# Two-layer graph attention: score rows spread by GpSimd's broadcast in place of transfers from HBM, and the deviation by log, exp and a Newton step

## The chip, the cores and the metric

The kernel runs on one core of one Trainium2 chip. The metric is the device time in microseconds. A profile is one further execution, recorded by the hardware profiler; its span is a little longer than the timed median.

## The reference

A batch of 32 graphs with 512 nodes and 512 features each. The input is normalized by rows, passed through a relu and then through two layers of graph attention, and the result is added to the input. Cut to what matters:

```python
def gat_layer(x, mask, W, a_src, a_dst, bias, concat):
    xl = (x @ W).reshape(B, N, H, F)
    asrc = jnp.einsum('bnhf,hf->bnh', xl, a_src)
    adst = jnp.einsum('bnhf,hf->bnh', xl, a_dst)
    e = jax.nn.leaky_relu(asrc[:, :, None, :] + adst[:, None, :, :], 0.2)
    e = jnp.where(mask[..., None], e, -1e9)
    attn = jax.nn.softmax(e, axis=1)                    # over the sources
    out = jnp.einsum('bsdh,bshf->bdhf', attn, xl)
    return (out, heads joined or averaged) + bias

h = relu((x - mean(x)) / sqrt(var(x) + 1e-5))           # by rows
h = elu(gat_layer(h, mask, W1, ...))                    # 4 heads of 256
return x + gat_layer(h, mask, W2, ...)                  # 1 head of 512
```

The mask is `adj > 0` with the diagonal added. All is float32.

## The kernel before, in words

All 32 graphs are worked one after the other, with up to three in flight at once. For each graph the kernel does this:

- `load` (L548) and `norm` (L586) bring in x and compute mean and deviation by rows: bn_stats and bn_aggr on VectorE, then the power -0.5 of variance plus epsilon on GpSimd (L597), which takes a constant tile `half`. `norm_turn` (L606) applies it with a relu on ScalarE and turns the tile, from the third graph on through a transposing transfer (`x<-adj`, L637) with a copy on ScalarE before and after it.
- `masks` (L555) makes a mask of 0 and a large negative number in `m`, writes it to HBM (`dm`) and turns it (`mt`).
- `project1` and `project2` (L962, L1158) are the products with the weights, and `gather1` and `gather2` (L1079, L1251) the products with the attention. They work by a scheme of seven half-size products in place of eight, so that VectorE forms sums and differences of blocks (`hs`, `t`, `p`, `xl`, `h`), and PSUM (`mm`) is emptied by ScalarE and VectorE. Matmuls are recorded under L439.
- The scores of a layer are in `Soft` (L657). For each destination `first` (L710) adds the source scores to a destination's score, with the leaky relu (ScalarE, `l<-as,z`), applies the turned mask and takes the largest (VectorE, `l<-l,mt`), and sums the exponentials (ScalarE, `l<-l,low`); from that come two rows per head. `second` (L763) then builds the attention with the sources on the partitions: VectorE takes the larger of two sums of these rows (`p<-rr,z`), GpSimd issues an accumulating transfer that adds the mask from HBM (`p<-dm`, L433, two per head), and ScalarE takes the exponential (`p<-p,z`).

**The spread.** In two places a vector that lies with 128 nodes down the partitions has to become one long row that every partition holds: the source scores (tile `as`, two heads at once, or one in layer 2) and the two rows of the softmax (tile `rr`, once per head). Both go through `Soft.spread` (L665). VectorE transposes the vector in blocks of 32 (`as<-z`, `rr<-low`), a small transfer writes it to HBM (`das<-as`, `drr<-rr`), and a second one reads it back to all 128 partitions (`as<-das`, `rr<-drr`). Per graph there are three spreads of scores and five of softmax rows, most of them 1024 elements long. There are two `as` tiles and two `rr` tiles. The readers are ScalarE (`l<-as,z`) and VectorE (`p<-rr,z`).

**What sets the order of the work.** Nothing is issued while the functions run: each operation is added to a `Program` (L87) with an engine, a price in us, what it reads and writes, and for transfers a size in us. `order` (L234) then plans all engines together and emits the instructions in the planned order. Every engine runs its own list strictly in that order. TensorE's list is the order of the calls; the others are chosen by rank. Waits between engines are priced by

```python
CROSS, SAME = 0.15, 0.07
PAIRS = {("PE", "ACT"): 0.21, ("PE", "DVE"): 0.21, ("DVE", "POOL"): 0.58, ("POOL", "DVE"): 0.4}
DMA_LEAD, DMA_TAIL, AHEAD = 0.8, 2.0, 3.5
```

and jobs of SyncE and GpSimd are held back while the planned transfers run more than `AHEAD` us behind (L220). The plan knows nothing of one engine holding up another at the memory. So a change of one price or of one operation moves instructions everywhere on ScalarE, VectorE, GpSimd and SyncE. Operations are recorded under the helpers' lines: ScalarE L422, VectorE L425, transfers of SyncE L428, accumulating transfers of GpSimd L433.

Of the kernel before, what the change touches and what calls it, by code (L numbers as in the profile page):

```python
# [10 lines left out]
F32 = mybir.dt.float32  # L11
# [3 lines left out]
AF = mybir.ActivationFunctionType  # L15
OP = mybir.AluOpType
# [3 lines left out]
P = 128  # L20
EPS = 1e-5
# [277 lines left out]
def tile_gat(  # L299
# [36 lines left out]
    nc = tc.nc  # L336
# [4 lines left out]
    NT = N // P  # L341
# [9 lines left out]
    sbuf = ctx.enter_context(tc.tile_pool(name="sbuf", bufs=1))  # L351
# [6 lines left out]
    def slots(name, n, shape, dtype=F32, pool=sbuf):  # L358
# [4 lines left out]
    make_identity(nc, identf)  # L363
    diag = sbuf.tile([P, P], BF16, name="diag")
    nc.vector.tensor_scalar(diag, identf, -1.0, BIG, op0=OP.add, op1=OP.mult)
    half = sbuf.tile([P, NT], F32, name="half")
    nc.vector.memset(half, -0.5)

# [19 lines left out]
    m = sbuf.tile([P, NT, N], BF16, name="m")  # L390
# [17 lines left out]
                tensor=w1_sb.tensor, offset=w1_sb.offset + NT * (DO + 2) + i * NT * N,  # L408
                ap=[w1_sb.ap[0], [N, NT], [1, N]],
# [9 lines left out]
    prog = Program()  # L419

    def act(cost, reads, writes, *a, **k):
        prog.add("ACT", cost, reads, writes, lambda: nc.scalar.activation(*a, **k))  # L422

    def dve(cost, reads, writes, f, *a, **k):
        prog.add("DVE", cost, reads, writes, lambda: f(*a, **k))  # L425

    def dma(size, reads, writes, to, at, cost=0.4):
        prog.add("SP", cost, reads, writes, lambda: nc.sync.dma_start(to, at), size)  # L428
# [15 lines left out]
    COPY, ADD, TINY = 0.28, 0.34, 0.1  # L444
# [141 lines left out]
    def norm(b):  # L586
        sk, st = stats.take()
        S, A = nc.vector.BN_STATS_DIM, nc.vector.BN_AGGR_DIM
        for t, (xk, xt) in enumerate(XT[b]):
            dve(0.61, [xk], [sk + (t,)], nc.vector.bn_stats, st[:, t, :S], xt)  # L590
            dve(TINY, [sk + (t,)], [sk + (t,)], nc.vector.bn_aggr, st[:, t, S : S + A], st[:, t, :S])
        every = [sk + (t,) for t in range(NT)]
        rstd = st[:, :, S + A]
        dve(TINY, every, every, nc.vector.tensor_scalar_add, rstd, st[:, :, S + 1], EPS)
        prog.add(
            "POOL", 1.0, every, every,
            lambda: nc.gpsimd.tensor_tensor(rstd, rstd, half, op=OP.pow),  # L597
        )
        shift = st[:, :, S]
        dve(  # L600
            TINY, every, every, nc.vector.scalar_tensor_tensor,
            shift, shift, -1.0, rstd, op0=OP.mult, op1=OP.mult,
        )
        ST[b] = sk, st
# [52 lines left out]
    class Soft:  # L657
# [7 lines left out]
        def spread(self, v, keys, rows, to, through, n=NT):  # L665

            k = rows * n
            ok, o = to.take()
            dk, dr = through.take()

            c = 32 // k
            sb = o[:, 0, :32]
            dve(
                0.12, keys, [ok], nc.vector.transpose,
                sb, bass.AP(tensor=v.tensor, offset=v.offset, ap=[v.ap[0], [1, k], [0, c]]),
            )
            dma(
                0.03, [ok], [dk], dr[:k].rearrange("k (b j) -> b k j", j=32),
                bass.AP(
                    tensor=sb.tensor, offset=sb.offset, ap=[[c * sb.ap[0][0], P // c], [1, 32]]  # L680
                ),
                0.55,
            )
            dma(
                0.18 * rows * n, [dk], [ok], o[:, :rows, : n * P],
                bass.AP(tensor=dr.tensor, offset=dr.offset, ap=[[0, P], [n * P, rows], [1, n * P]]),
            )
            through.give(dk)
            return ok, o

        def columns(self, i, given=None):

# [173 lines left out]
    def sevens(left, right, rkeys, put, kh, units, width, order, seeds={}):  # L866
# [3 lines left out]
        for us, n in order:  # L870
# [30 lines left out]
            if n in (2, 3, 4):  # L901
# [17 lines left out]
                tensor=hs.tensor, offset=hs.offset + KQ * M,  # L919
                ap=[hs.ap[0], [KH * M, 2], [M, 2], [1, M]],  # L920
# [398 lines left out]
    load(0)  # L1319
    weights1()  # L1320
    norm(0)
    for t in range(NT):
        norm_turn(0, t)
# [3 lines left out]
    run(project1_first(given))  # L1327
    load(1)
    norm(1)
    for t in range(NT):  # L1330
        norm_turn(1, t)
# [16 lines left out]
    for h in gather1_plain(S1[0], range(H)):  # L1348
# [8 lines left out]
        if h == 2:  # L1357
            s.second(1)
    load(2)
    norm(2)  # L1360
    s.first(2)
    s.first(3)
# [8 lines left out]
    for i in range(B - 1):  # L1371
# [17 lines left out]
        if front:  # L1389
# [5 lines left out]
            n = S1[i + 2] = Soft(i + 2, 1, scores_1)  # L1395
# [69 lines left out]
```

## Time and profile before

The time is 2844.79 us, the median of three runs from 2837.85 to 2845.18. The profiled execution has a span of 2856.3 us.

| from the page | value |
|---|---|
| packets of all transfers | 501.42 MB, mean 176 GB/s |
| queue q1 (SyncE's transfers) | 332.15 MB, 42.5% of 16 engines' span |
| queue q0 (GpSimd's transfers) | 166.74 MB, 25.6% |
| rr<-drr | 159 transfers of 512 KB and 2 of 256 KB |
| as<-das | 64 transfers of 512 KB and 32 of 256 KB |
| p<-dm | 314 transfers of 512 KB, median 5.6 us to landing |
| VectorE p<-rr,z, 128x512 | 740 ns mean, 636 times (some shorter) |
| VectorE l<-l,mt, 128x512 | 682 ns mean, 640 times |
| GpSimd stats<-stats,half | 1512 ns mean, 32 times |

How to read it: a busy share is busy time over the span. In a line of a group or a wait, `p<-rr,z` means that the instruction writes tile p and reads rr and z, and `engine line <- other` means that the engine stood idle before its instruction until the other was done. PE is TensorE, DVE VectorE, ACT ScalarE, POOL GpSimd and SP SyncE. The chain of waits is followed back from the last instruction, at each step to what released it. Since each engine's list is fixed, a late landing also delays everything that stands behind the instruction that waits for it.

### The profile page before, as it was taken

How to read it: one execution, taken by the hardware profiler on the slowest of the kernel's cores; microseconds unless marked ns; L12 is line 12 of the kernel's file. 1: busy time of each engine (PE TensorE's matmuls, PEld its weight loads, DVE VectorE, ACT ScalarE, POOL GpSimd, SP SyncE). 2: the span in 40 equal slices, each digit the busy share in tenths (PEclk: the TensorE clock that was granted, in tenths of full speed). 3: DMA queues.
4: the chain of work that ended last, by engine and by line, in shares of the span. 5: the costliest groups of instructions: out<-in, count | busy, mean ns of one | idle time of the engine just before them, and what ended most of it. 6: DMA issues, size and time to landing. Idle time of an engine off the chain costs nothing.

```text
span 2856.3 us, 39591 instructions
## 1 busy us (share of the span) xinstructions
PE 2770.0 (97%) x12520; PEld 2373.9 (83%) x12520; DVE 2432.2 (85%) x5494; ACT 2384.9 (83%) x4506; POOL 322.6 (11%) x356
## 2 busy tenths in 40 slices
PE   7999999999999999999999999999999999999988
PEld 6688888888888888888888888888878888888876
DVE  7888898888898878879889888888878988888885
ACT  5888898878898888878888888888878898888882
POOL 0111111101111101111011100111101111111110
PEclk9999999999999999999999999999999999999999
DMA  7666767666777667776687776777666767666652
GB/s 226 153 176 167 204 161 188 181 174 170 189 188 177 176 166 196 167 173 179 172 181 167 196 155 184 170 176 197 164 168 178 195 174 178 183 183 177 176 141 96
DMA packets 369077, 501.42 MB, mean 176 GB/s; under 512 B 220260, under 2 KB 225124, under 8 KB 368868
## 3 DMA queue, kind: packets, MB, share of 16 engines
q1 hardware_dynamic: 323076, 332.15, 42.5%
q0 software_dynamic: 45792, 166.74, 25.6%
q8 instruction: 100, 1.64, 0.2%
q14 instruction: 109, 0.89, 0.1%
HBM read 315.89 MB, written 51.31 MB: 129 GB/s over the span
## 4 chain that ended last, share of the span: by engine, by line
PE 79%; DMA 9%; ACT 5%; DVE 5%; issue 2%; SPq 0%; POOL 0%; ACTq 0%; POOLq 0%; DVEq 0%
PE mm L439 79%; DMA p<-dm 4%; DMA x<-adj 3%; DVE p L425 1%; ACT l L422 1%; ACT p L422 1%; DMA as<-das 1%; ACT adj L422 1%; ACT ht L422 1%; DVE l L425 1%; DVE t L425 1%; DVE hs L425 1%; DVE h L425 1%; ACT xl L422 0%; ACT xr L422 0%
## 5 line engine op out<-in xcount | busy, mean ns | idle before, releaser
L439 PE MATMUL mm<-w_sb,hs 128*128 128x257 f32 (+2 forms) x3032 | 685.3, 383 | 25.1 <-ACT h L422 16.1
L439 PEld LDWEIGHTS mm<-w_sb,hs 128*128 128x128 f32 x3032 | 576.1, 191 | 120.7 <-ACT h L422 20.1
L433 POOL DMA_DIRECT2D p<-dm x314 | 274.4, 878 | 2420.4 <-DVE p L425 1459.7
L422 ACT ACTIVATE l<-l,low 128x512 f32<-128x512 f32 x640 | 455.2, 713 | 40.0 <-DVE low L425 39.3
L439 PE MATMUL mm<-w_sb,ht 128*128 128x258 f32 x2112 | 482.6, 382 | 3.6 <-ACT ht L422 1.4
L425 DVE CUSTOM_DVE_ANT_1 l<-l,mt 128x512 f32<-128x512 f32 x640 | 425.2, 682 | 62.8 <-ACT l L422 62.2
L422 ACT ACTIVATE p<-p,z 128x512 f32<-128x512 f32 (+1 forms) x636 | 424.7, 709 | 62.3 <-DMA p<-dm 51.2
L439 PE MATMUL mm<-p,xl 128*128 128x256 f32 (+1 forms) x1984 | 470.6, 385 | 4.5 <-ACT h L422 3.0
L422 ACT ACTIVATE l<-as,z 128x512 f32<-128x512 f32 x640 | 436.9, 712 | 32.0 <-DMA as<-das 30.7
L439 PE MATMUL mm<-w_sb,h 128*128 128x257 f32 x2056 | 459.5, 380 | 3.3 <-DVE w_sb L425 3.3
L425 DVE SCALAR_TENSOR_TENSOR p<-rr,z 128x512 f32<-128x512 f32 (+1 forms) x636 | 448.1, 740 | 15.8 <-DMA rr<-drr 15.1
L439 PEld LDWEIGHTS mm<-w_sb,ht 128*128 128x128 f32 x2112 | 398.8, 190 | 67.6 <-ACT xl L422 3.3
L439 PEld LDWEIGHTS mm<-w_sb,h 128*128 128x128 f32 x2056 | 390.3, 190 | 62.3 <-DVE w_sb L425 3.7
L439 PEld LDWEIGHTS mm<-p,xl 128*128 128x128 f32 x1984 | 377.8, 191 | 68.0 <-issue 6.9
L422 ACT ACTIVATE xr<-h,b_sb 128x512 f32<-128x512 f32 x248 | 171.8, 714 | 120.9 <-DVE h L425 120.9
L422 ACT ACTIVATE xl<-mm 128x516 f32<-128x516 f32 (+2 forms) x376 | 218.4, 586 | 46.9 <-PE mm L439 45.6
L439 PE MATMUL mm<-t,hs 128*128 128x256 f32 x992 | 233.1, 386 | 25.0 <-ACT mm L422 22.0
L439 PEld LDWEIGHTS mm<-t,hs 128*128 128x128 f32 x992 | 189.7, 193 | 57.5 <-ACT mm L422 27.1
L425 DVE SCALAR_TENSOR_TENSOR h<-h,b_sb,xr 128x512 f32<-128x512 f32 x248 | 181.5, 744 | 46.5 <-ACT xr L422 46.4
L422 ACT ACTIVATE ht<-x 128x1024 uint16<-128x1024 uint16 x120 | 159.3, 1351 | 30.2 <-DMA x<-adj 30.2
L439 PE MATMUL mm<-xl,p 128*128 128x256 f32 (+1 forms) x752 | 180.2, 388 | 2.3 <-DVE t L425 1.6
L422 ACT ACTIVATE h<-mm 128x512 f32<-128x512 f32 (+1 forms) x256 | 146.3, 574 | 26.5 <-PE mm L439 24.4
(113 smaller groups left out, 3268.0 us busy)
## 6 DMA issues: line engine op xcount, KB each, us to landing
p<-dm POOLq DMA_DIRECT2D x314, 512.0 KB, 5.6
rr<-drr SPq DMA_DIRECT2D x159, 512.0 KB
x<-in_x_dram SPq DMA_DIRECT2D x128, 256.0 KB
adj<-in_adj_dram SPq DMA_DIRECT2D x128, 256.0 KB
as<-das SPq DMA_DIRECT2D x64, 512.0 KB
t<-in_x_dram SPq DMA_DIRECT2D x62, 512.0 KB
out_dram<-t SPq DMA_DIRECT2D x60, 512.0 KB
dm<-m SPq DMA_DIRECT2D x32, 512.0 KB
```

The source lines that it names most:

```text
L422: prog.add("ACT", cost, reads, writes, lambda: nc.scalar.activation(*a, **k))
L425: prog.add("DVE", cost, reads, writes, lambda: f(*a, **k))
L433: lambda: nc.gpsimd.dma_start(to, at, accum_op=OP.add), size,
L439: f(*a, **k)
```

## The change

In `spread` the row is read back from HBM into one partition only, and GpSimd copies it from there to all 128 by `partition_broadcast`. This is to take the large transfers out of the DMA queues. The power on GpSimd goes at the same time: the reciprocal of the deviation is now exp(-0.5 log v) on ScalarE, with one Newton step on VectorE after it, in a column of the statistics tile that is no longer needed. The transpose on VectorE and the small write to HBM stay. The tile is now addressed flat, with a row of the last graph's half-size spreads lying right behind the other.

```diff
-    half = sbuf.tile([P, NT], F32, name="half")
-    nc.vector.memset(half, -0.5)
...
-        dve(TINY, every, every, nc.vector.tensor_scalar_add, rstd, st[:, :, S + 1], EPS)
-        prog.add(
-            "POOL", 1.0, every, every,
-            lambda: nc.gpsimd.tensor_tensor(rstd, rstd, half, op=OP.pow),
-        )
+        v, a = st[:, :, S + 1], st[:, :, 0]
+        dve(TINY, every, every, nc.vector.tensor_scalar_add, v, v, EPS)
+        act(0.25, every, every, rstd, v, AF.Ln)
+        act(0.25, every, every, rstd, rstd, AF.Exp, scale=-0.5)
+        dve(TINY, every, every, nc.vector.tensor_mul, a, rstd, rstd)
+        dve(TINY, every, every, nc.vector.tensor_mul, a, a, v)
+        dve(TINY, every, every, nc.vector.tensor_scalar, a, a, -0.5, 1.5, op0=OP.mult, op1=OP.add)
+        dve(TINY, every, every, nc.vector.tensor_mul, rstd, rstd, a)
...
+            flat = bass.AP(tensor=o.tensor, offset=o.offset, ap=[o.ap[0], [1, k * P]])
             dma(
-                0.18 * rows * n, [dk], [ok], o[:, :rows, : n * P],
-                bass.AP(tensor=dr.tensor, offset=dr.offset, ap=[[0, P], [n * P, rows], [1, n * P]]),
+                0.03, [dk], [ok], flat[0:1],
+                bass.AP(tensor=dr.tensor, offset=dr.offset, ap=[[0, 1], [1, k * P]]),
+            )
+            prog.add(
+                "POOL", 0.25 + 0.85 * k / 8, [ok], [ok],
+                lambda: nc.gpsimd.partition_broadcast(flat, flat[0:1]),
             )
             through.give(dk)
-            return ok, o
+            return ok, flat.rearrange("p (r m) -> p r m", r=rows)
```

## The prediction

> **What bounds the kernel now.** I read the page's busy shares first, then the table by stretches, then the chain, then the groups and waits that carry it. The page's first part and the head of its chain:
>
> ```profile
> PE 2770.0 (97%) x12520; PEld 2373.9 (83%) x12520; DVE 2432.2 (85%) x5494; ACT 2384.9 (83%) x4506; POOL 322.6 (11%) x356
> ...
> PE 79%; DMA 9%; ACT 5%; DVE 5%; issue 2%; SPq 0%; POOL 0%; ACTq 0%; POOLq 0%; DVEq 0%
> PE mm L439 79%; DMA p<-dm 4%; DMA x<-adj 3%; DVE p L425 1%; ACT l L422 1%; ACT p L422 1%; DMA as<-das 1%; ACT adj L422 1%; ACT ht L422 1%; DVE l L425 1%; DVE t L425 1%; DVE hs L425 1%; DVE h L425 1%; ACT xl L422 0%; ACT xr L422 0%
> ```
>
> TensorE is the bound: 2770 of 2856 us. The change touches none of its matmuls, so the most that any relief can win is its 86 us of idle time. The table by stretches (engine busy us and instruction counts, granted clock, DMA share) says where that idle time is:
>
> ```profile
> 0.00:150.00 150.00, 127.69 (x508) 96.61 (x509) 121.49 (x386) 104.14 (x202) 17.21 (x24) 0.98 0.72 190
> 150.00:2720.00 2570.00, 2523.10 (x11530) 2185.16 (x11529) 2218.76 (x4906) 2209.53 (x4152) 295.85 (x321) 1.00 0.70 178
> 2500.00:2720.00 220.00, 219.02 (x1009) 190.74 (x1008) 190.51 (x416) 191.87 (x358) 24.62 (x27) 1.00 0.65 176
> 2720.00:2857.00 137.00, 119.21 (x485) 92.09 (x483) 91.99 (x203) 71.22 (x153) 9.52 (x11) 0.97 0.41 120
> ```
>
> 22 us at the start, 18 at the end, 47 in the 2570 us between. And where TensorE has no idle time at all (2500 to 2720), VectorE and ScalarE are both 87% busy: neither has much room. The list of waits (total us, times, longest):
>
> ```profile
> ACT p L422 <- DMA p<-dm: 51.2, 31, 9.8
> ACT l L422 <- DMA as<-das: 30.7, 24, 5.1
> ACT ht L422 <- DMA x<-adj: 30.2, 9, 8.2
> PE mm L439 <- ACT mm L422: 24.1, 17, 5.4
> PE mm L439 <- ACT h L422: 19.7, 12, 5.6
> ```
>
> TensorE stands still when ScalarE, in order, sits before an exponential or a copy whose transfer has not landed, and so brings a PSUM copy (mm, h) late: 44 us of the 86. The landings that hold it are the mask accumulation p<-dm and the transpose x<-adj; of the rows that the change removes, as<-das holds ScalarE for 31 us and rr<-drr holds VectorE for 15.
>
> [...] the only GpSimd instruction that reads here, the power (ns min/median/max):
>
> ```profile
> L597 POOL TENSOR_TENSOR stats<-stats,half x32: 1036/1404/2277, 7.2 to 2655.1; 128x4 f32<-128x4 f32 x32
> ```
>
> Its shortest, 1036 ns, is the first, at 7.2 us, with VectorE idle; the median is 0.37 us longer and the longest 1.24, about one VectorE instruction (0.68 to 1.22 us): GpSimd waits its turn. The other side, VectorE held by GpSimd, no row shows[...]. [...]
>
> **The change, part by part.**
>
> *Transfers removed.* 223 spreads of 512 KB and 34 of 256 KB: 126 of 501 MB. Queue q1 takes 42.5% of the DMA time for 332 MB, a part of it in the small packets of the transposes, so this is at most 126/332 x 42.5 = 16 points and I take 10 to 16: the share falls from 0.68 to between 0.52 and 0.58. What it can give back is time in which landings hold ScalarE. If the hold shortens with the load, a fifth of 44 us is 9; I count 9, and half (22 us) as the most.
>
> *Transfers added.* 257 of 4 or 2 KB into one partition. Small transfers cost, in the tail, 1.6 us (das issued 2811.93, the read that waits for it 2813.56) and under load up to 3.6 (1569.37 to 1573.02). The large read took 3.5 us in the tail (2813.56 to the ScalarE instruction at 2817.02) and up to 6.9 under load (1573.02 to 1579.90). [...] Start and end have some five spreads on the path: about 4 us won.
>
> *Broadcasts added.* In 1024-element equivalents 223 + 34/2 = 240. [...] What it costs is VectorE. Its rows with two SBUF inputs (p<-rr,z 448.1 us, l<-l,mt 425.2, h<-h,b_sb,xr 181.5, and the sums and differences of p, t, xl, hs, h, x, ht) are about three quarters of its time. [...]
>
> *A queue.* A broadcast waits at the head of GpSimd's queue for its row to land, and the accumulations p<-dm (318, 0.88 us each) stand behind it; ScalarE's exponentials wait for those. In the built order one or two broadcasts stand between pairs of accumulations. Before, these waited for VectorE's p alone. A row that lands 1 to 3 us later than planned now delays a mask too. Most have room: ScalarE waited in 31 of 636 exponentials. I give 0 to 10 us, and take 3.
>
> *Deviation.* Removed: 32 powers, 48.4 us of GpSimd. Added: 64 ScalarE instructions on 128x4 at 0.195 us (the low<-low row: 31.4 us for 161), 12 us; 128 small VectorE instructions at about 0.155 us (the low<-low row: 153 ns), 20 us. They belong to a batch that TensorE reaches much later; the work of the current one hides their latency, not their engine time. At the start VectorE waits for weights behind the same rows anyway (1.86 us idle before 8.99), so nothing is taken there.
>
> *From engine time to the end.* TensorE's order of instructions is the same. VectorE gets 158 + 20 = 178 us more, 2610 of 2856 us, 91%; in the stretch where TensorE never stops that is 13.7 us onto 29.5 us of idle time. Half of VectorE's slack goes. Its idle time is pinned to waits on ScalarE and TensorE, and a hold falls at any moment, so not all is absorbed: I take a quarter as reaching TensorE (ends: none and six tenths; this is a judgement). 178 x 0.25 = 45, ScalarE's 12 x 0.25 = 3, the queue 3, less 9 and 4 won: +38 us. 2845 + 38 = 2883, rounded to 2880.
>
> **The rivals.**
>
> *Relief wins (faster).* VectorE is not held, or absorbs it: then half of the 44 us of ScalarE-held idle time comes back, and 4 at the ends, less 3 to 5 for the small instructions: 2845 - 22 = 2823. For it: every large idle time of TensorE in the middle leads back to a landing, and a quarter of the bytes goes. Against it: the transposes and the accumulations, which hold ScalarE longest, stay as they are.
>
> *A wash.* As spreads were planned with their latency hidden (31 + 15 us of waiting in all for 257), their going frees nothing on the path, and a light hold takes the 9 us back: 2845.
>
> *GpSimd's price is the high one.* 396 us of holding makes VectorE 2848 us busy, as long as the whole kernel; it is then the bound, with its own waits on top: 2960 or more.
>
> **How the numbers follow.** Held VectorE, 2880: 0.48. Relief, 2823: 0.37. Wash: 0.11. High price: 0.04. The first is likeliest because [...] the power's lengthening shows one side of it, while the largest landings are untouched; it is not safer because VectorE's slack may swallow everything. A few of the relief cases end within 0.3%. Faster 0.37, same 0.12, slower 0.51. The held case runs, with none to six tenths reaching the end, from about 2840 to 2845 + 107 + 6 - 13 = 2945; relief at its best, all 44 us and the ends, is near 2805. Leaving out the outer tenth on each side: 2808 to 2938.
>
> **What would show each step.** Right: VectorE rows with two SBUF inputs grow longer or get idle time before them beside a broadcast, VectorE's busy plus held time nears 2600 us, TensorE's waits name VectorE (t, h, hs, xl) instead of ScalarE; the DMA share falls to 0.52 to 0.58[...]. Wrong: those rows keep their 0.68 and 0.74 us; then the hold is absent and the relief case stands. If ACT p <- DMA p<-dm falls well below 51 us, relief is larger than I count; if it grows, the accumulations are stuck behind broadcasts.

## The result, and the profile after

The changed kernel takes 2884.06 us (median of four runs, 2883.0 to 2888.96) against 2844.98 for the kernel before (2837.85 to 2855.34): a ratio of 1.0138, interval 1.0104 to 1.0171. It is slower, by 39 us. The forecast was 2880.

The page's first part of the changed kernel, and of its queues the one that carried the spreads:

```profile
PE 2779.4 (96%) x12520; PEld 2361.5 (82%) x12520; DVE 2575.3 (89%) x5621; ACT 2394.4 (83%) x4570; POOL 645.9 (22%) x581
...
q1 hardware_dynamic: 286326, 207.29, 26.7%
```

VectorE is busy for 143 us more than before, GpSimd for 323 more, and q1 moves 207 instead of 332 MB. The page's chain breaks off after a few per cent of the span in this profile, so it is not used. The table by stretches of the changed kernel (columns as before):

```profile
0.00:150.00 150.00, 126.74 (x507) 94.55 (x508) 131.18 (x398) 106.69 (x210) 32.10 (x33) 1.00 0.57 147
150.00:2720.00 2570.00, 2507.78 (x11405) 2151.95 (x11404) 2326.90 (x4974) 2191.66 (x4160) 589.80 (x524) 1.00 0.52 132
2720.00:2882.70 162.70, 144.86 (x610) 115.04 (x609) 117.18 (x251) 96.09 (x202) 24.04 (x24) 0.99 0.33 92
```

In the 2570 us between, TensorE's idle time went from 47 to 62 us and the DMA share from 0.70 to 0.52. At the two ends it is 23.3 and 17.8 us, as before (22.3 and 17.8): nothing was won there.

**The waits changed sides.** From the list of waits of the changed kernel, and the group of its exponentials (busy us, mean ns, idle before it with what ended it):

```profile
ACT l L420 <- DVE low L423: 71.0, 94, 2.9
ACT mm L420 <- DVE t L423: 66.9, 33, 4.3
ACT l L420 <- POOL as L692: 45.3, 27, 4.9
PEld mm L437 <- DVE h L423: 32.0, 39, 1.9
PE mm L437 <- DVE h L423: 20.0, 27, 1.5
```

```profile
L420 ACT ACTIVATE p<-p,z 128x512 f32<-128x512 f32 (+1 forms) x636 | 427.1, 708 | 20.9 <-DVE p L423 10.6 <-DMA p<-dm 10.2
```

Two rows of the same list before the change:

```profile
ACT l L422 <- DVE low L425: 39.3, 49, 1.7
ACT mm L422 <- DVE t L425: 35.0, 25, 2.4
```

Before, ScalarE waited 51.2 us for the landing of the mask accumulation; now 10.2. Before, it waited 39.3 us for VectorE's `low` and 35.0 for `t`; now 71.0 and 66.9. TensorE's list of waits led to ScalarE's copies; now VectorE's `h` stands among its first.

**VectorE was held.** The same rows of the kernel before and then of the changed one, from the views by tile (times, ns min/median/max, first and last start):

```profile
L425 DVE TENSOR_TENSOR xl<-xl,mm x187: 641/684/694, 63.3 to 2807.4; 128x516 f32<-128x516 f32 x124, 128x514 f32<-128x514 f32 x63
L425 DVE TENSOR_TENSOR xl<-xl x94: 415/683/694, 131.0 to 2767.0; 128x512 f32<-128x512 f32 x90, 128x256 f32<-128x256 f32 x4
L425 DVE COPY z<-xl x62: 126/164/189, 131.7 to 2811.5; 128x4 f32<-128x4 f32 x62
...
L425 DVE CUSTOM_DVE_ANT_1 l<-l,mt x640: 642/683/694, 41.6 to 2824.7; 128x512 f32<-128x512 f32 x160
```

```profile
L423 DVE TENSOR_TENSOR xl<-xl,mm x187: 636/681/694, 55.9 to 2833.8; 128x516 f32<-128x516 f32 x124, 128x514 f32<-128x514 f32 x63
L423 DVE TENSOR_TENSOR xl<-xl x94: 410/680/1644, 130.8 to 2796.2; 128x512 f32<-128x512 f32 x90, 128x256 f32<-128x256 f32 x4
L423 DVE COPY z<-xl x62: 126/160/1269, 130.6 to 2837.9; 128x4 f32<-128x4 f32 x62
...
L423 DVE CUSTOM_DVE_ANT_1 l<-l,mt x640: 641/681/1648, 42.5 to 2851.1; 128x512 f32<-128x512 f32 x160
```

The medians stay; the longest of a row are 0.95 to 1.1 us longer in the rows shown, but only where both inputs, or the one input of a copy, come from SBUF. Where one input is a product in PSUM (`xl<-xl,mm`), no instruction is longer at all. Counted in the trace against each row's median, 214 VectorE instructions were lengthened, by 151 us in all: 123 us in instructions with two inputs, 28 in copies and in operations with a scalar (TENSOR_SCALAR). In the kernel before, none was lengthened by more than 0.06 us. The broadcasts themselves:

```profile
L692 POOL PARTITION_BROADCAST rr<-rr x161: 798/1424/3680, 61.0 to 2859.0; - x161
L692 POOL PARTITION_BROADCAST as<-as x96: 794/1299/4132, 37.6 to 2841.5; - x96
```

0.79 us at the shortest, 1.3 to 1.4 in the median. The eight of 0.79 to 0.80 us start with VectorE idle, on an instruction that reads PSUM, or in the last 0.14 us of one from SBUF; in the longest, 4.13 us, five TENSOR_TENSOR from SBUF and a TENSOR_SCALAR of VectorE run from start to end. GpSimd waits its turn too.

**What TensorE lost, by size.** The product instructions are the same 12,520 in every kernel, 0.216 us apart when nothing holds them. Counting in each trace what every start came later than that, sorted by the single delay, gives the table on which most of what follows rests. Its sums differ between kernels by as much as the spans of their profiles do (154.8 less 128.0 is 26.8; 2882.7 less 2856.3 is 26.4). That is less than the 39 us between the medians, since the profile of the kernel before is of an execution of 2858 us, 13 above its median. "Products at half clock" are those that came about 0.43 us apart while the clock granted to TensorE was halved:

| us lost | before | changed |
|---|---|---|
| delays over 3 us | 30.7 (7) | 13.1 (3) |
| 1.5 to 3 us | 16.6 (8) | 19.8 (11) |
| 0.5 to 1.5 us | 29.4 (34) | 64.1 (73) |
| under 0.5 us | 36.8 (207) | 51.8 (318) |
| products at half clock | 14.5 (66) | 6.0 (27) |
| sum | 128.0 | 154.8 |

So the change did two things. It took away more than half of the long stops, 18 us, with 8 us of a kind that the prediction did not count: products at half the clock. And it put in 53 us of shorter delays. The half clock is seen in the table by stretches of the kernel before, cut around one stop of TensorE (at 585.4, 2.7 us):

```profile
584.00:588.60 4.60, 1.92 (x9) 1.36 (x8) 1.92 (x4) 2.97 (x5) 0.86 (x1) 1.00 1.09 328
588.60:592.00 3.40, 3.40 (x9) 2.67 (x8) 3.10 (x9) 2.98 (x7) 0.00 (x0) 0.50 0.84 233
592.00:595.40 3.40, 3.40 (x17) 2.96 (x16) 2.33 (x7) 3.17 (x9) 0.00 (x0) 0.99 0.50 121
```

In the 3.4 us after the stop the granted clock is 0.50 and 9 products pass, in the next 3.4 us 17. So it was after most long stops, and not after all: in the trace of before, eight of its nine stops over 2.3 us had 3.4 or 6.8 us at 0.50 that began during the stop or within 1.2 us of its end, none of the five from 1.6 to 1.9 us had.

### The profile page after: what moved, and what is told of

The parts are those of the page before. It is cut to its first block, busy times and chain, and to the rows that moved or that the text cites. A ratio compares the mean times of both kernels' runs of the same rounds, so it can differ in the third digit from the quotient of the medians.

```text
span 2882.7 us, 40624 instructions
## 1 busy us (share of the span) xinstructions
PE 2779.4 (96%) x12520; PEld 2361.5 (82%) x12520; DVE 2575.3 (89%) x5621; ACT 2394.4 (83%) x4570; POOL 645.9 (22%) x581
## 5 line engine op out<-in xcount | busy, mean ns | idle before, releaser
L437 PEld LDWEIGHTS mm<-w_sb,hs 128*128 128x128 f32 x3032 | 573.0, 190 | 128.5 <-ACT h L420 15.1
L423 DVE CUSTOM_DVE_ANT_1 l<-l,mt 128x512 f32<-128x512 f32 x640 | 447.0, 714 | 52.9 <-ACT l L420 52.5
L423 DVE SCALAR_TENSOR_TENSOR p<-rr,z 128x512 f32<-128x512 f32 (+1 forms) x636 | 469.9, 770 | 7.1 <-POOL rr L692 7.1
L420 ACT ACTIVATE l<-as,z 128x512 f32<-128x512 f32 x640 | 437.1, 712 | 46.8 <-POOL as L692 45.3
L692 POOL PARTITION_BROADCAST rr<-rr x161 | 251.1, 1565 | 942.9 <-DMA rr<-drr 606.4
L420 ACT ACTIVATE xl<-mm 128x516 f32<-128x516 f32 (+2 forms) x376 | 217.9, 585 | 31.7 <-PE mm L437 30.7
L692 POOL PARTITION_BROADCAST as<-as x96 | 137.0, 1427 | 448.4 <-DMA as<-das 188.9
L423 DVE SCALAR_TENSOR_TENSOR h<-h,b_sb,xr 128x512 f32<-128x512 f32 x248 | 196.5, 806 | 28.3 <-ACT xr L420 28.1
```

The source lines that it names most:

```text
L692: lambda: nc.gpsimd.partition_broadcast(flat, flat[0:1]),
```

## The experiments

Ratios are to the kernel before on the same chip; one point is 1%, about 28.5 us. The medians of the kernel before there were 2854.56 to 2856.58.

### The hold: no broadcast, one, two

**no_hold** is the changed kernel, its order unchanged, with a write of the row's tile where the broadcast was: GpSimd is busy at the same place, the readers wait for it in the same way, but nothing is read from SBUF. A write is about half a microsecond shorter than a broadcast (1.03 us in the mean for `rr`, against 1.57); the next run makes up for that. The rows' values are lost; products that nothing holds stay 0.216 us apart.

```diff
-                lambda: nc.gpsimd.partition_broadcast(flat, flat[0:1]),
+                lambda: nc.gpsimd.memset(flat, 0.0),
```

> The changed kernel with its plan and order, but where GpSimd broadcasts a row it fills the row's tile with zeros (a memset of the same size, about 1.2 us: it waits for the same transfer, is waited for by the same readers and writes as much, but reads nothing). The rows are thus never spread and the attention is computed from zeros. Hold theory: no VectorE row lengthened by more than a few us in all, and the 1.4% goes: ratio to the kernel before 0.985 to 1.000 (the relief of 28 us, less the 14 us of the new deviation). Rival 'queue and lateness' (GpSimd's queue and the later rows carry the loss): ratio stays 1.010 to 1.017.

Measured: 2796.25 us, ratio 0.9792 (0.9757 to 0.9826). Its page's first part, and the writes' group:

```profile
PE 2752.4 (98%) x12520; PEld 2368.6 (85%) x12520; DVE 2442.4 (87%) x5621; ACT 2393.3 (86%) x4570; POOL 503.9 (18%) x581
```

```profile
L692 POOL MEMSET rr<- 128x1024 f32 (+1 forms) x161 | 165.6, 1031 | 951.5 <-DMA rr<-drr 621.0 <-DVE p L423 61.5 <-DVE low L423 54.1
```

This is below the range that was expected with the hold gone (0.985 to 1.000); what that means for the rest of the change is taken up further down. VectorE is 133 us less busy than with the broadcast (2575.3 less 2442.4), in the same 5621 instructions. Instructions with two inputs from SBUF were lengthened by 3 us in all, in place of 123. The time falls by 1.0138 - 0.9792 = 3.5 points, 98 us; between the two profiles TensorE's loss falls from 154.8 to 71.0, 84 us. So two thirds to three quarters of VectorE's held time came out at the end; the intervals of the two ratios leave about 14 us to either side of the 98.

**no_hold_twice** writes the tile twice. It asks whether it is the reading or simply GpSimd's time and the later row that cost.

```diff
-                lambda: nc.gpsimd.partition_broadcast(flat, flat[0:1]),
+                lambda: [nc.gpsimd.memset(flat, 0.0) for _ in range(2)],
```

> As no_hold with two memsets in place of one: the counterpart of twice without any reading. It has twice's lateness (some 1.2 us more for each row) and its fuller GpSimd queue. Hold theory: twice's rise of about 5 points over the changed kernel is mostly hold, so this one is under 2 points over no_hold. Rival: lateness and queue make it 4 to 6 points over no_hold.

Measured: 2803.99 us, 0.9818 (0.9782 to 0.9853): 8 us above one write, with overlapping intervals, for 229 us more of GpSimd (732.9 against 503.9). Each row comes about 0.9 us later and hardly anything follows: ScalarE's wait for `as` grows from 22.0 to 58.4 us, and TensorE's loss from 71.0 to 74.4. The changed kernel has less of both, 645.9 us of GpSimd and 45.3 us of waiting for `as`, and takes 3.2 points more. So for the changed kernel the rival falls that the later row or GpSimd's time, not the held engine, makes the loss.

**twice** broadcasts twice.

```diff
-                lambda: nc.gpsimd.partition_broadcast(flat, flat[0:1]),
+                lambda: [nc.gpsimd.partition_broadcast(flat, flat[0:1]) for _ in range(2)],
```

> The changed kernel with every broadcast run twice; plan and order as in the changed kernel. Hold theory: VectorE rows lengthen by 270 to 320 us in all, double the 151 us of the changed kernel, and the time rises by 60 to 120 us over it. Rival 'a row's lateness alone': each row is 1.4 us later, most have room: 5 to 25 us.

Measured: 3050.17 us, 1.0656 (1.0617 to 1.0695). That is 5.2 points, 148 us, above the changed kernel, more than expected. 435 instructions were lengthened by 313 us, twice the 151. The page and a wait of it:

```profile
PE 2832.5 (93%) x12520; PEld 2373.9 (78%) x12520; DVE 2736.2 (90%) x5621; ACT 2396.8 (79%) x4570; POOL 1026.9 (34%) x838
```

```profile
PE mm L437 <- DVE h L423: 67.8, 46, 3.7
```

161 us more of VectorE, and 148 us more of time (166 between the two profiles), where a second write costs 8 us. This is not the hold alone. A second broadcast takes longer than a second write (381 us more of GpSimd, against 229), and its rows come later, as the same wait shows in twice and then in no_hold_twice:

```profile
ACT l L420 <- POOL as L692: 140.4, 56, 7.2
ACT l L420 <- POOL as L692: 58.4, 37, 4.7
```

How much of the 148 us is hold and how much is the later row was not separated.

### The relief: no large transfers, all of them, or none taken away

**relief_only** is the kernel before with its own order, but the row is read back into one partition and never spread; the other partitions keep zeros.

```diff
+    for o in (*ass.tiles, *rrs.tiles):
+        nc.gpsimd.memset(o, 0.0)
...
-                0.18 * rows * n, [dk], [ok], o[:, :rows, : n * P],
-                bass.AP(tensor=dr.tensor, offset=dr.offset, ap=[[0, P], [n * P, rows], [1, n * P]]),
+                0.18 * rows * n, [dk], [ok], o[0:1, :rows, : n * P],
+                bass.AP(tensor=dr.tensor, offset=dr.offset, ap=[[0, 1], [n * P, rows], [1, n * P]]),
```

> The kernel before with its plan and order, but every spread row is landed in one partition only and never spread (the other partitions keep the zeros of the start, so the attention is computed from wrong rows): 126 MB of transfers less, no broadcast. Worth of the relief alone. My step: 9 us and at most 22, so 2823 to 2840 us; DMA share 0.52 to 0.58; ACT p <- DMA p<-dm clearly under 51 us. Rival 'wash': 2842 to 2850.

Measured: 2823.07 us, 0.9902 (0.9862 to 0.9942): 28 us won, three times what the prediction counted. TensorE's loss falls from 128.0 to 97.1: 11 us in delays over 3 us, 7 in those from 1.5 to 3, 8 in those under 0.5, and 4 at half clock. The two waits of TensorE from which the prediction had its 44 us are now:

```profile
PE mm L441 <- ACT mm L424: 13.9, 11, 5.7
PE mm L441 <- ACT h L424: 10.3, 8, 6.2
```

24 us in place of 44: nearly half went, not the fifth that the prediction took from the share of the load. The rest of the gain lies elsewhere, some of it in slow products that go with a stop.

**full_transfer** is the changed kernel and its order with the large transfer kept ahead of the broadcast.

```diff
-                0.03, [dk], [ok], flat[0:1],
-                bass.AP(tensor=dr.tensor, offset=dr.offset, ap=[[0, 1], [1, k * P]]),
+                0.03, [dk], [ok], flat,
+                bass.AP(tensor=dr.tensor, offset=dr.offset, ap=[[0, P], [1, k * P]]),
```

> The changed kernel with its own plan and order, but each row is read back into all partitions (the large transfer) before GpSimd broadcasts it over itself: the hold and the queue stay, the relief of the 126 MB is taken away. If relief is worth what relief_only showed (about 28 us), 1.0 to 1.5% above the changed kernel: some 2915 to 2935 us. Rival 'the relief does nothing in the changed kernel, since VectorE is the bound there': within 8 us of the changed kernel's about 2890.

Measured: 2964.6 us, 1.0353 (1.0312 to 1.0394), 2.15 points or 61 us above the changed kernel, more than expected. Two of its waits:

```profile
ACT l L420 <- POOL as L692: 172.8, 70, 6.2
DVE p L423 <- POOL rr L692: 81.0, 52, 4.8
```

They were 45.3 and 7.1 us. In this order the large transfers can be expected to cost more than in the old one, since it was planned without them (they are still priced at 0.03 us) and a broadcast follows each. On the other side VectorE was lengthened by only 120 us here, against 151, which hides a part of their cost. So 61 us is not a clean price of the relief in the new order, nor a sure upper end of it; 28 us is what it is worth in the old.

**landing_price** takes nothing away: the kernel before, with the accumulating transfer told to the plan as 2.8 us in place of 2.2.

```diff
-                            2.2, keys + [mk], keys,
+                            2.8, keys + [mk], keys,
```

> The kernel before, but the plan prices an accumulating transfer at 2.8 in place of 2.2 us, since p<-dm lands 5.6 us after its issue in the profile; the rest is as before. If the landings hold ScalarE because the plan expects them too early, a part of the 28 us of relief_only comes without taking any transfer away: ratio 0.992 to 0.998. If the plan has no room to wait: 1.000 to 1.008.

Measured: 2830.2 us, 0.9897 (0.9857 to 0.9936). The group of the exponentials:

```profile
L422 ACT ACTIVATE p<-p,z 128x512 f32<-128x512 f32 (+1 forms) x636 | 426.1, 708 | 26.9 <-DMA p<-dm 16.3 <-DVE p L425 10.6
```

The wait for the mask's landing falls from 51.2 to 16.3 us, and TensorE's loss to 87.5 (in a profiled execution of 2817.5 us, 13 under the median), with 501 MB still moved. It is faster than both kernels, by as much as taking 126 MB away, and a little more than expected. But another wait for a landing grew:

```profile
ACT l L422 <- DMA as<-das: 83.6, 43, 5.2
```

It was 30.7 us. ScalarE's waits for the masks, the turned blocks (`x<-adj`) and these rows together went only from 112 to 100 us. What is shown is that another order, got by one number, can win 28 us with the load unchanged; that it wins because landings are no longer looked for too early is not shown.

### The deviation

**norm_only** has the new deviation alone; rows are spread by transfers as before.

```diff
-        prog.add(
-            "POOL", 1.0, every, every,
-            lambda: nc.gpsimd.tensor_tensor(rstd, rstd, half, op=OP.pow),
-        )
+        act(0.25, every, every, rstd, v, AF.Ln)
+        act(0.25, every, every, rstd, rstd, AF.Exp, scale=-0.5)
...
+        dve(TINY, every, every, nc.vector.tensor_mul, rstd, rstd, a)
```

> Only the deviation is changed (log, exp, Newton step); rows are spread by large transfers as before. Hold theory (VectorE is held while a broadcast reads): no broadcast, so 2840 to 2856 us, at most 10 us over the kernel before, VectorE busy about 2452 us with no row lengthened. Rival 'small instructions': the 192 added instructions carry the loss, 2870 us or more.

Measured: 2869.88 us, 1.0048 (1.0024 to 1.0071), 14 us, more than the hold theory allowed. No VectorE instruction is lengthened. But the waits moved in a place that has nothing to do with the deviation:

```profile
ACT ht L420 <- DMA x<-adj: 61.1, 18, 11.2
ACT p L420 <- DMA p<-dm: 28.4, 23, 3.2
```

They were 30.2 and 51.2: with the new operations the plan has another order of everything.

**small_ops** tells instruction time from order: the kernel before in its own order, with four small VectorE and two small ScalarE instructions per graph on a tile of their own, attached to the deviation's jobs after planning.

```diff
+    def more_dve(f):
+        f()
+        for _ in range(3):
+            nc.vector.tensor_mul(tiny[:, 0], tiny[:, 1], tiny[:, 1])
+        nc.vector.tensor_scalar(tiny[:, 0], tiny[:, 1], -0.5, 1.5, op0=OP.mult, op1=OP.add)
+
+    def more_act(f):
+        for _ in range(2):
+            nc.scalar.activation(tiny[:, 2], tiny[:, 1], AF.Exp)
+        f()
```

> The kernel before with its plan and order; beside each graph's power (which stays) VectorE runs four more instructions and ScalarE two more on a tile of 128x4 that nobody needs: the number and size of the small instructions of the new deviation, without a new plan. If norm_only's 14 us is the time of these instructions: ratio 1.003 to 1.007. If it is the other order that the plan chose: ratio within 0.998 to 1.002.

Measured: 2850.9 us, 0.9977 (0.995 to 1.0004). The instructions cost nothing that can be measured. Norm_only's 14 us are those of the other order, or of what its chain of dependent operations asks of that order; these two were not separated.

### A wrong experiment, and what it showed

**hold_only** was to price the hold in the order without broadcasts: norm_only, and behind 240 of the 318 accumulating transfers four broadcasts of 256 elements on a tile that nobody reads.

```diff
+            nc.gpsimd.dma_start(to, at, accum_op=OP.add)
+            sent[0] += 1
+            if sent[0] * 240 // 318 > (sent[0] - 1) * 240 // 318:
+                for _ in range(4):
+                    nc.gpsimd.partition_broadcast(junk, junk[0:1])
```

> norm_only with its plan, rows by large transfers; behind 240 of the 318 accumulating transfers GpSimd also runs four broadcasts of 256 elements on a scratch tile that nobody waits for. No latency is added to any row and no transfer is taken away. Hold theory: VectorE rows with two SBUF inputs lengthen by 100 to 200 us in all, and the time is 25 to 55 us above norm_only. Rival 'queue and latency' (rows come late through GpSimd's queue): within 8 us of norm_only.

Measured: 2949.56 us, 1.0334 (1.0293 to 1.0375), 80 us above norm_only, far more than expected. 597 instructions were lengthened by 125 us, but ScalarE's wait for the mask's landing also rose from 28.4 to 98.2 us, which a hold of VectorE does not explain. Two runs put other work in the same place.

**write_only** has four writes of the same tile in place of the four broadcasts (0.31 us each at the shortest, where the broadcast of 256 has 0.55):

```diff
-                    nc.gpsimd.partition_broadcast(junk, junk[0:1])
+                    nc.gpsimd.memset(junk, 0.0)
```

> As hold_only, but with four memsets of 128x256 in place of each four broadcasts: GpSimd is busy for about as long and writes, but reads nothing. Hold theory (it is the reading that holds VectorE): VectorE rows with two inputs keep their length, 0 to 8 us above norm_only. Rival 'any GpSimd work costs' (its queue, or its writes): 20 us or more above norm_only, as hold_only.

Measured: 2865.21 us, 1.0028 (1.0011 to 1.0045): not slower than norm_only. Then **write_long**, with ten writes, about 3.1 us of queue as the broadcasts had:

```diff
-                for _ in range(4):
+                for _ in range(10):
```

> As write_only, but ten memsets of 128x256 (0.31 us each in write_only) in place of four, so that GpSimd's queue is held for about the 3 us that the four broadcasts of hold_only took, and still nothing is read. If hold_only's 80 us came from accumulations stuck behind GpSimd's work (rival 'queue'), this one is 40 us or more above norm_only too. If they came from the reading (hold theory), it stays within 15 us of norm_only, with less than 20 us of lengthened VectorE rows.

Measured: 2962.56 us, 1.0353 (1.0309 to 1.0396), with only 12.6 us of lengthening. Two of its waits:

```profile
ACT p L423 <- DMA p<-dm: 170.3, 96, 5.6
PE mm L444 <- ACT mm L423: 59.2, 35, 5.4
```

So 3 us on GpSimd's queue that the plan knows nothing of push the next accumulation back and cost 3 points over norm_only with hardly any hold. Hold_only's loss mixes the two and says nothing of the hold's price. In the changed kernel the broadcasts have a price and a place in the plan; there the same wait is 10.2 us.

### The plan told of the hold

**told** is the changed kernel with truer prices: 1.4 us for a broadcast of 1024 and 0.5 us taken from VectorE at its start.

```diff
+            prog.holds[len(prog.jobs)] = 0.5 * k / 8
             prog.add(
-                "POOL", 0.25 + 0.85 * k / 8, [ok], [ok],
+                "POOL", 0.4 + 1.0 * k / 8, [ok], [ok],
```

and where the plan places a job:

```diff
+            if j in self.holds:
+                free["DVE"] = max(free["DVE"], t) + self.holds[j]
```

> The changed kernel, but the plan is told: a broadcast costs 0.4 + 1.0 us on GpSimd for 1024 elements and takes 0.5 us of VectorE at the same moment. Nothing else differs. If part of the loss is that the plan packs VectorE without knowing of the hold, 5 to 25 us below the changed kernel. If the hold's time itself is what costs (VectorE and ScalarE have no room to give), within 5 us of it.

Measured: 2882.61 us, 1.0077 (1.0051 to 1.0103), 0.6 points under the changed kernel; the median itself is only 1.5 us under it, on another chip, so this is a small gain at best. 166 us of lengthening are still there, and TensorE's loss is 151.0 against 154.8. No delay over 3 us is left, but 89.3 us in delays of 0.5 to 1.5: with these prices the plan shifted the hold and did not avoid it.

## Why the prediction was right

The sum was right to 4 us by luck: two of its terms were both much too small, with opposite signs. The mechanism of the loss, VectorE held by the broadcast's reads, was right, but it was assumed: in the kernel before no VectorE instruction is lengthened by more than 0.06 us. Point by point:

- **The bound** held: TensorE stayed at 96%, its loss went from 128 to 155 us, and the whole effect came through it. Its weakness: "the most that any relief can win is its 86 us of idle time" left out the products at half clock and delays hidden in busy time. The profile had shown it: a granted clock of 0.98 and 0.97 at the two ends stood in the table that the prediction quotes.
- **The broadcast**: what one takes was not shown by any trace of the kernel before. Measured 0.79 us at the shortest, 1.3 to 1.4 in the median, and GpSimd busy for 646 us. The high price, with 396 us of holding and VectorE busy for 2848, is out: 133 to 151 us and 2575.
- **The hold**: the forecast of 158 us in which VectorE waits for GpSimd's reads was an assumption that no trace of the kernel before shows. 133 to 151 were measured, and 123 of the 151 in instructions with two inputs, the rows that were named. The step "three quarters of its time" was off in kind only: copies and TENSOR_SCALAR were lengthened as well, by 28 us, and `z<-xl` shows it (0.16 us in the median, up to 1.27).
- **"I take a quarter as reaching TensorE"**: this step failed. Measured two thirds to three quarters (84 to 98 us of 133). The term is 84 to 98 us where the sum had 45 for the hold and the small instructions. The end given for it, six tenths, was too low as well. The prediction saw that VectorE has 14% of idle time and that this is pinned to waits; it did not draw the consequence that held time may then be added between two waits and not taken from idle time. The larger waits for `low`, `t` and `h` fit this; no run shows it by itself.
- **Relief, "a fifth of 44 us is 9; I count 9, and half (22 us) as the most"**: failed. It was 28 us in the old order. The waits did not shrink with the share of the load: of the 44 us nearly half went (20), and the slow products were not counted. ACT p <- DMA p<-dm fell from 51 to 10, the sign named beforehand for a relief larger than counted.
- **The share of DMA time**, 0.52 to 0.58: 0.52, right.
- **Start and end, 4 us won**: this rested on an assumed time of the broadcast. Nothing was won; the idle time at the ends is 23.3 and 17.8 us against 22.3 and 17.8. A shorter spread is not seen elsewhere either: ScalarE's wait for `as` rose from 30.7 to 45.3 us, VectorE's for `rr` fell from 15.1 to 7.1.
- **The queue, 3 us**: the landing waits did not grow, so nothing of it is seen in the planned place; no_hold_twice gives at most some 8 us for a doubled queue and later rows together.
- **Deviation**, 3 us for ScalarE and 5 of VectorE's: as instruction time nothing (small_ops); as a change of order 14 us (norm_only). The mechanism was wrong.

Against +39 us: with the broadcast's reading taken out and the order kept, the kernel takes 59 us less than the one before (no_hold, 0.9792), or about 98 us less than the changed one. So the hold is worth some +98 us, and everything else in the change together -59, where the prediction had -7 for all but the hold and VectorE's small instructions. Of these -59 the relief is 28 in the old order. The other 31, or 45 if the deviation costs its 14 us in this order too, are open: the relief may be worth more in an order that was planned with it, or the new order may be better in itself, as that of landing_price was by 28 us. full_transfer does not decide between them. Without the hold no delay of TensorE over 3 us is left (no_hold 71.0 us lost, of that 2.8 at half clock), but told has none either, with the hold. Of the rivals, the relief case had a gain of the right kind and its counterweight wrong; the wash and the high price are out.

## What to carry to other kernels

When transfers are moved to GpSimd, count the VectorE time that its reads of SBUF take (here 151 us for 257 broadcasts), and where the bound engine is fed by VectorE through chains of short waits, reckon with most of it as lost (here two thirds to three quarters), not with a share of the idle time. Count long stops of TensorE with the slow products behind them (14.5 us in the kernel before), and look for them in the granted clock before the busy shares. And where a plan fixes the order of everything, try other prices in it before taking load away: one number won here what 126 MB did. A kernel with its own order kept (no_hold, relief_only) prices a change; one with a new order prices the order too.

## What was not expected of the hardware

- The halving of TensorE's clock goes with no one length of stop. Counted over the traces of all fourteen kernels, stops with the clock halved during them or within 3.5 us after them: 48 of 49 over 3.4 us, 47 of 72 from 2.3 to 3.4, 9 of 24 from 1.95 to 2.3, and 3 of 50 from 1.6 to 1.95 (in the kernel before and the changed one together 6 of 7, 5 of 6, none of that length, and 0 of 8). Of TensorE's loss 14.5 us lie there in the kernel before, 6.0 in the changed kernel and 36.8 with two broadcasts.
- A VectorE copy of four elements per partition took up to 1.27 us beside a broadcast (0.16 in the median), and `xl<-xl,mm` with an input in PSUM never more than 0.694.
- A write by GpSimd lengthens VectorE instructions a little too: 21 us in no_hold, 41.5 in no_hold_twice, against 151 with the broadcast. But it meets others: 16 of the 21 us lie in copies and TENSOR_SCALAR, and 3 in instructions with two inputs, against 28 and 123 with the broadcast.
- A broadcast of 256 elements takes 0.55 us at the shortest and one of 1024 0.79, so four small ones cost nearly three times one large.
